# A decoder layer in one launch: parts of the output product fetched three ahead, expert outputs in tiles of their own, four splits moved to GpSimd

## The chip, the cores and the metric

The kernel runs on one core of one Trainium2 chip. The metric is the device time of one launch in microseconds (us), as the median of several runs. A core has five engines with an instruction queue each: TensorE (PE, matrix products; its weight loads are listed apart as PEld), VectorE (DVE), ScalarE (ACT), GpSimd (POOL) and SyncE (SP, which here issues most DMA transfers). An engine works through its queue in order; a semaphore wait holds everything behind it on that engine.

## What is computed

A decoder layer over 16 batches of 100 tokens of width 512 (1600 tokens), with an encoder context of 361 tokens for each batch, to float32's accuracy. Cut to what matters:

```python
x = layernorm(x + self_attention(x))                 # 16 heads of 32, causal
q, k, v = x @ Wq + bq, ctx @ Wk + bk, ctx @ Wv + bv  # 16 query heads, 4 key/value heads, width 128
o = softmax(rms(q) @ rms(k).T / sqrt(128) + mask) @ v
x = layernorm(x + o @ Wo)                            # Wo: 2048 x 512

logits = x @ router_w + router_b                     # 8 experts
vals, idx = top_k(logits, 2)
g = softmax(vals)
h = silu(x @ expert_w[e] + expert_b[e])              # for the two experts e of each token
y = x + (sum of g * h) @ proj_w + proj_b
x = layernorm(x + norm_w * y / rms(y))
```

## The kernel before, in words

**Accuracy.** PE multiplies float32r numbers. Each float32 operand is held as a `Pair` of two float32r tiles, high and low. `split` (L120) makes it: the high part is a copy on ScalarE (L124), the low part is source less high on VectorE or GpSimd (L127). `mm3` (L129) makes a product of two pairs from three matmuls (high-high, high-low, low-high; L131, L132, L133).

**Order of the work.** The kernel is written in the Tile framework. Python code emits operations in an order written out by hand. A planner then puts each engine's instructions into an order by a timeline that it estimates; semaphores are put in where tiles depend on one another. A pool has a fixed number of buffers for each tag; a new tile waits until the last readers and writers of the buffer that it takes are done. A pool that is opened in memory that a closed pool held waits likewise for the users of that memory.

**Stages.** Self attention (to about 350 us); its output product and the cross attention's queries (to about 600); cross attention (to about 1136); its output product with layer norm and router; experts; the weighted sum, projection and last norms.

**Cross attention.** For each batch and each of four groups of four heads: `x_scores` (scores of a head, L131 to L133; mask and maximum on VectorE, L679; exponential on ScalarE, L690; sums' reciprocal; normalisation on GpSimd, L692), `x_turn` (transposes of a chunk of encoder tokens, L700, then a split), `x_attend` (product with values; then the group's output goes to the DRAM scratch `od`, laid out by tiles of 128 tokens). The steps of two neighbouring groups are interleaved by a hand-written list. In batches before the last, the keys and values of the next batch are projected among them.

**Output product.** There are 13 tiles of tokens (the last has 64) and four groups of `Wo`, so 52 parts. Tiles 0 to 9 come tile by tile; of the last three (`TAIL`) the parts come by weight group. `d_load(i)` fetches a part from `od` by a DMA on SP (L755) into tile `of` and splits it into the pair `ot`; the low part goes to VectorE for odd `i`, to GpSimd for even `i`. `of` and `ot` have two buffers each, in pool `d_in`. `d_part(i)` issues its 12 matmuls of 128x512 into a PSUM bank (`acc`). `d_norm` (L779) adds the residual and normalises; `d_turn` transposes the normalised tile (L865) for the router. The first four parts are issued among the groups of the last batch; the others come in the main loop (L1252), which loads part i+1 and then multiplies part i. Weights of experts are fetched and split among them (`load_expert`; low parts `WL` on GpSimd).

**Router.** `d_logits` adds a tile's products with the router weights. `choose` takes each token's two experts. At the cut (`CUT`, tile 9) `settle` and `slots` work out, from the first nine tiles, the expert's tokens for 11 slot tiles of 128 tokens each, in many small VectorE operations that end in `is_in` (L1156); small products on PE (L1171) make the index lists. The other slots are settled after the last tile.

**Experts.** There are 32 slot tiles. `e_gather` (L1195) fetches a slot's 128 tokens by an indirect DMA on GpSimd's queue into tile `xs` (pool `k_x`, five buffers). `e_turn` transposes it (four PE transposes, L1206) and splits the result; `e_product` issues 12 matmuls with the weights of the slot's expert (`ph`); `e_out` adds the bias on VectorE (L1230), with its result written over the gathered tile `xs`, applies Silu on ScalarE (L1231), and SP writes the tile to the DRAM scratch `ysd` (L1232). For the weighted sum, rows of `ysd` are gathered for each tile of tokens (`y`, L1377, on GpSimd's queue).

Of the kernel before, what the change touches and what calls it, by code (L numbers as in the profile page):

```python
# [29 lines left out]
NG = B // GB  # L30
GT = GB * S
TT = [(t, min(128, T - t)) for t in range(0, T, 128)]  # tiles of all tokens
# [5 lines left out]
def pieces(t0, n):  # L38
    """The batches that tokens t0 to t0 + n lie in: (batch, its token, offset, count)."""
    out, t = [], t0  # L40
    while t < t0 + n:
        b, r = divmod(t, S)
        m = min(S - r, t0 + n - t)
        out.append((b, r, t - t0, m))
        t += m
    return out


class Pair:
    """A float32 array as the exact sum of two that float32r holds."""  # L50
# [12 lines left out]
def tile_decoder_layer(  # L63
# [29 lines left out]
    # Exp and Ln of one table serve both attentions.  # L93
# [26 lines left out]
    def split(dst, src, high=None, low=None):  # L120
        """dst, a pair, from src."""
# [7 lines left out]
    def mm3(out, a, b, start, stop):  # L129
        """The product of two pairs, to float32's accuracy."""  # L130
# [8 lines left out]
    def rsqrt(v, p, n, name, p_=None):  # L139
        """1 / sqrt(v), from the activation tables, with one Newton step."""  # L140
# [33 lines left out]
    # Eight slots of 512 rows by 512 columns, each a pair: weights, and what fits  # L174
    # beside them.
# [9 lines left out]
    def split_rows(dst, src, name, high=None, low=None):  # L185
        """Weights from DRAM into a pair, by rows."""
# [48 lines left out]
    def chunk(n, c, queue=None):  # L235
        """Weights from DRAM, 128 columns (of queries or keys) or rows (of values)."""
# [18 lines left out]
    # Keys of four heads, each in its own block of rows and of columns.  # L255
# [8 lines left out]
    # Added to negated scores: zero up to the diagonal, BIG past it.  # L264
# [35 lines left out]
    def self_q(g, c):  # L300
# [3 lines left out]
        # The scores come out negated and scaled.  # L304
# [71 lines left out]
    def self_attend(g, c, r):  # L376
# [3 lines left out]
        # Of each head's rows only its own columns are its output.  # L380
# [48 lines left out]
    LA = 3  # items that scores are ahead by  # L429
    extra = {}  # what comes with an item  # L430
# [1276 lines left out]
```

## Time and profile before

| what | value |
|---|---|
| three runs | 1482.58, 1488.05, 1488.45 us; median 1488.05 |
| span of the profiled execution (its own time is not listed beside it) | 1484.0 us |
| mean granted PE clock | 0.972 |
| attention's last groups, 1078.0 to 1136.5 | PE busy 58.50 of 58.5 us |
| first output tiles, 1136.5 to 1180 | PE busy 35.76 of 43.5 us |
| output tiles, 1180 to 1226 | PE busy 44.78 of 46 us |
| the cut, 1226 to 1270 | PE busy 33.49 of 44 us |
| experts among the second settling, 1270 to 1319 | PE busy 45.64 of 49 us |
| experts, 1319 to 1396 | PE busy 65.64 of 77 us |
| experts and weighted sums, 1396 to 1440 | PE busy 42.07 of 44 us |
| the end, 1440 to 1484 | PE busy 23.23 of 44 us |

The span runs from the first to the last instruction of one profiled execution; it lies within the range of the three runs. "Granted clock" is the share of its full clock that the throttle let PE have. The profile also tells, for each idle stretch of an engine, which instruction or transfer released it ("<-"): a line such as "acc<-WH,ot_l" gives output and inputs of an instruction by the program's names.

### The profile page before, as it was taken

To read this page: it belongs to the slowest core of one execution; us is meant where nothing else is said; L and a number is where in the kernel's file an instruction comes from. 1 tells how busy PE (TensorE), PEld (TensorE's weight loads), DVE (VectorE), ACT (ScalarE), POOL (GpSimd) and SP (SyncE) were. 2 spreads that over 40 slices of the span, in tenths; PEclk is the share of its full clock that TensorE was granted. 3 is DMA by queue.
4 is the path that set the end of the run, shared out by engine and by line. 5 is a ranking of instruction groups with operands and counts; after the bars stand their busy time and mean duration, and the time that the engine had idled before them with its cause. 6 is when DMAs were issued, how large, how long until landed. Compare 5 with 4: busy or idle time off the path is not lost.

```text
span 1484.0 us, 24770 instructions
## 1 busy us (share of the span) xinstructions
PE 1391.4 (94%) x7248; PEld 1139.8 (77%) x7248; DVE 1018.2 (69%) x3523; ACT 813.3 (55%) x2164; POOL 731.9 (49%) x853
## 2 busy tenths in 40 slices
PE   7999999999999999999999999999999898798985
PEld 6777786788877888788788788788887676576763
DVE  5775766677676777777777677677745558752698
ACT  5766877444444566566666566566654233332453
POOL 6455545534424555455655555555544444442643
PEclk9999999999999999999999999999999999899997
DMA  4011015456544222122322322321435645666774
GB/s 130 34 46 62 22 36 145 144 142 118 125 97 92 74 65 80 44 64 64 89 61 64 87 63 63 93 60 45 99 107 142 207 164 159 191 213 184 253 232 146
DMA packets 197875, 159.77 MB, mean 108 GB/s; under 512 B 133322, under 2 KB 152878, under 8 KB 197742
## 3 DMA queue, kind: packets, MB, share of 16 engines
q1 hardware_dynamic: 187904, 137.83, 33.7%
q0 software_dynamic: 4576, 14.95, 3.3%
q10 hardware_dynamic: 5262, 5.41, 1.3%
q8 instruction: 60, 0.98, 0.3%
q14 instruction: 73, 0.60, 0.1%
HBM read 107.16 MB, written 50.99 MB: 107 GB/s over the span
## 4 chain that ended last, share of the span: by engine, by line
PE 67%; DVE 17%; DMA 7%; issue 4%; ACT 3%; POOL 1%; SPq 1%; DVEq 0%; POOLq 0%; ACTq 0%
PE pv L131 4%; PE pv L132 4%; PE pv L133 4%; PE pq L131 4%; PE ptp L700 4%; PE pq L132 4%; PE pq L133 3%; PE s L131 3%; PE s L133 3%; PE s L132 3%; PE pk L131 3%; PE pk L133 3%; PE pk L132 3%; DVE ksq L639 2%; PE av L383 2%
## 5 line engine op out<-in xcount | busy, mean ns | idle before, releaser
L692 POOL TENSOR_SCALAR p<-p,sums 100x361 f32<-100x361 f32 x256 | 146.7, 577 | 107.7 <-DVE sums L691 88.7
L679 DVE CUSTOM_DVE_ANT_0 p<-s,nmask 100x361 f32<-100x361 f32 x256 | 133.5, 527 | 73.6 <-PE s L133 71.5
L690 ACT ACTIVATE p<-p,nm 100x361 f32<-100x361 f32 x256 | 153.4, 602 | 47.2 <-DVE nm L679 44.1
L127 DVE TENSOR_TENSOR pT_l<-ptp,pT_h 128x400 fp32r<-128x400 f32 (+1 forms) x192 | 107.4, 567 | 58.3 <-ACT pT_h L124 58.1
L124 ACT CAST pT_h<-ptp 128x400 fp32r<-128x400 f32 (+1 forms) x192 | 91.5, 488 | 33.4 <-PE ptp L700 32.8
L700 PE MATMUL ptp<-ident,p 100*128 100x100 f32 (+1 forms) x768 | 108.2, 253 | 0.1
L700 PEld LDWEIGHTS ptp<-ident,p 100*128 100x128 f32 (+1 forms) x768 | 95.9, 152 | 15.5 <-POOL p L692 4.2
L127 POOL TENSOR_TENSOR cT_l<-cf,cT_h 128x512 fp32r<-128x512 f32 (+1 forms) x48 | 54.4, 1134 | 97.2 <-ACT cT_h L124 95.9
L133 PE MATMUL acc<-WH,ot_l 128*128 128x512 f32 (+1 forms) x208 | 86.2, 415 | 8.4 <-DVE ot_l L127 5.4
L131 PE MATMUL acc<-WH,ot_h 128*128 128x512 f32 (+1 forms) x208 | 85.8, 413 | 3.5 <-ACT ot_h L124 3.5
L127 POOL TENSOR_TENSOR WL<-qf,WH 128x400 fp32r<-128x400 f32 x64 | 67.3, 1051 | 43.5 <-ACT WH L124 39.7
L131 PE MATMUL s<-kT_h,WH 128*100 128x362 f32 x256 | 88.7, 357 | 0.0
L131 PE MATMUL av<-pT_h,WH 128*128 128x400 f32 (+1 forms) x192 | 76.7, 400 | 8.2 <-ACT pT_h L124 8.2
L132 PE MATMUL acc<-WL,ot_h 128*128 128x512 f32 (+1 forms) x208 | 84.4, 406 | 0.0
L133 PE MATMUL s<-kT_h,WL 128*100 128x362 f32 x256 | 84.1, 329 | 0.0
L132 PE MATMUL s<-kT_l,WH 128*100 128x362 f32 x256 | 83.7, 327 | 0.0
L131 PE MATMUL pq<-WH 128*128 128x512 f32 (+1 forms) x208 | 82.3, 396 | 0.1
L132 PE MATMUL pq<-WL,WH 128*128 128x512 f32 (+1 forms) x208 | 81.6, 394 | 0.5 <-POOL WL L127 0.5
L551 POOL TENSOR_TENSOR qs<-qs,r_q 128x512 f32<-128x512 f32 (+1 forms) x52 | 54.3, 1075 | 54.5 <-DVE r_q L155 25.5
L131 PE MATMUL pv<-WH,cT_h 128*128 128x512 f32 (+1 forms) x192 | 80.3, 418 | 0.8 <-DVE WL L127 0.8
L639 DVE CUSTOM_DVE_ANT_0 ksq<-ks 128x128 f32<-128x128 f32 (+1 forms) x192 | 78.3, 408 | 2.4
L360 POOL TENSOR_TENSOR p<-p,rinv 100x400 f32<-100x400 f32 x64 | 54.2, 855 | 51.8 <-DVE rinv L359 37.3
(349 smaller groups left out, 4407.3 us busy)
## 6 DMA issues: line engine op xcount, KB each, us to landing
qf<-qd SPq DMA_DIRECT2D x64, 200.0 KB, 2.6
of<-od SPq DMA_DIRECT2D x48, 256.0 KB, 3.5
cf<-in_ctxT SPq DMA_DIRECT2D x16, 722.0 KB, 4.2
eb<-in_expert_b SPq DMA_DIRECT2D x32, 256.0 KB, 3.8
ysd<-xs SPq DMA_DIRECT2D x32, 256.0 KB, 4.1
f_e<-in_expert_w SPq DMA_DIRECT2D x30, 256.0 KB, 4.5
f_wq<-in_Wq SPq DMA_DIRECT2D x16, 256.0 KB, 4.0
f_wo<-in_Wo SPq DMA_DIRECT2D x16, 256.0 KB, 4.6
```

The lines of the kernel that those rows point to most:

```text
L124: nc.scalar.copy(dst.h, src)
L127: low.tensor_tensor(dst.l, src, dst.h.bitcast(FP), ALU.subtract)
L131: nc.tensor.matmul(out, a.h, b.h, start=start, stop=False)
L132: nc.tensor.matmul(out, a.h, b.l, start=False, stop=False)
L133: nc.tensor.matmul(out, a.l, b.h, start=False, stop=stop)
L360: nc.gpsimd.tensor_tensor(p, p, rinv.unsqueeze(2).to_broadcast([S, 4, S]), ALU.mult)
L551: nc.gpsimd.tensor_tensor(qr[:, hs, :], qr[:, hs, :], rs[:n, hs].unsqueeze(2).to_broadcast([n, GR, HD2]), ALU.mult,)
L639: nc.vector.tensor_tensor_reduce(out=sq[:n], in0=kr[:, h, :], in1=kr[:, h, :], scale=1.0, scalar=0.0, op0=ALU.mult, op1=ALU.add, accum_out ...
L679: nc.vector.tensor_tensor_reduce(out=p, in0=sc[:, :SE], in1=nmask, scale=1.0, scalar=BIG, op0=ALU.add, op1=ALU.min, accum_out=nm,)
L690: nc.scalar.activation(p, p, AF.Exp, bias=nm, scale=-1.0, accum_out=sh)
L692: nc.gpsimd.tensor_scalar(p, p, sh, 1.0, ALU.mult, ALU.mult)
L700: nc.tensor.transpose(pt[:n, h, :], probs[h][:, c0 : c0 + n], ident[:S, :S])
```

## The change

Three things are changed, all after the cross attention. Comments are taken out too, and lines move by some.

1. `d_load` is divided. `d_fetch(i)` issues the DMA from `od`; `d_load(i)` splits what was fetched. In the main loop parts are fetched up to three ahead (`AHEAD`, with a counter `begun`). Odd parts are fetched into a second pool `d_in2` of two buffers, opened just before the main loop; even parts into `d_in`, as before. In the attention's last batch each fetch stands directly before its split.
2. The low split goes to GpSimd for every part of tiles 9 and 10, odd ones too (`by_pool`); so four more splits are on GpSimd. (`CUT` is defined further up for that.)
3. `e_out` writes into a tile `h` of its own (two buffers in pool `ebb`), not over `xs`; `xs` has four buffers, not five.

```diff
+    AHEAD = 3
+    CUT = NT - 4
...
+    def d_fetch(i):
+        t, g = parts[i]
+        n = TT[t][1]
+        p = inp["d2"] if "d2" in inp and i % 2 else inp["d"]
+        of = p.tile([128, GR, 128], FP, name=f"of_{t}_{g}", tag="of")
+        nc.sync.dma_start(of[:, :, :n], od[t][:, g * GR : (g + 1) * GR, :n])
+        OF[t, g] = of
+
     def d_load(i):
         t, g = parts[i]
         n = TT[t][1]
-        p = inp["d"]
-        of = p.tile([128, GR, 128], FP, name=f"of_{t}_{g}", tag="of")
-        nc.sync.dma_start(of[:, :, :n], od[t][:, g * GR : (g + 1) * GR, :n])
-        OT[t, g] = pair(p, [128, GR, 128], f"ot_{t}_{g}", tag="ot")
-        split(OT[t, g][:, :, :n], of[:, :, :n], low=nc.vector if i % 2 else nc.gpsimd)
+        of = OF.pop((t, g))
+        OT[t, g] = pair(inp["d"], [128, GR, 128], f"ot_{t}_{g}", tag="ot")
+        by_pool = i % 2 == 0 or CUT <= t < NT - TAIL + 1
+        split(
+            OT[t, g][:, :, :n], of[:, :, :n], low=nc.gpsimd if by_pool else nc.vector
+        )
...
-    xsp = pool(fin, "k_x", 5, side="right")
+    xsp = pool(fin, "k_x", 4, side="right")
...
     def e_turn(i):
-        xs = XG[i]
+        xs = XG.pop(i)
...
     def e_out(i):
         ph = PH.pop(i)
-        h = XG.pop(i)
+        h = ebb.tile([128, D], FP, name=f"h_{i}", tag="h", bufs=2)
         nc.vector.tensor_tensor(h, ph, EB.pop(i), ALU.add)
         nc.scalar.activation(h, h, AF.Silu)
         nc.sync.dma_start(ysd[i * 128 : (i + 1) * 128, :], h)
...
+    d2 = ExitStack()
+    inp["d2"] = pool(d2, "d_in2", 2)
+    begun = HEAD * NKV + 1
     for i in range(HEAD * NKV, len(parts)):
         t, g = parts[i]
+        while begun < min(i + 1 + AHEAD, len(parts)):
+            d_fetch(begun)
+            begun += 1
         if i + 1 < len(parts):
             d_load(i + 1)
...
+    d2.close()
     d_i.close()
```

More of the change, by code (lines that the diff above doesn't have):

```diff
@@ L739, in tile_decoder_layer @@
     order = [(b, g) for b in range(B) for g in range(NKV)]
-    OT, X1 = {}, {}
+    OT, OF, X1 = {}, {}, {}
+    AHEAD = 3
+    CUT = NT - 4
     def d_open():
@@ L798, in tile_decoder_layer @@
                 d_open()
+                d_fetch(0)
                 d_load(0)
             for j in range(HEAD * g, HEAD * (g + 1)):
+                d_fetch(j + 1)
                 d_load(j + 1)
@@ L898, in tile_decoder_layer @@
     NSL = NE + (2 * T - NE) // 128
-    CUT, EARLY = NT - 4, 11
+    EARLY = 11
     assert EARLY <= 2 * CUT - (NE - 1)
```

## The prediction, made before the result was known

> **What bounds the kernel now.** I read the page first: TensorE (PE) is busy 94% of the span and leads its chain (67%), so only time in which PE idles or is throttled can be won, and most of that lies after 1136 us, where the slices fall from 9 to 8 and 7.
>
> ```profile
> span 1484.0 us, 24770 instructions
> PE 1391.4 (94%) x7248; PEld 1139.8 (77%) x7248; DVE 1018.2 (69%) x3523; ACT 813.3 (55%) x2164; POOL 731.9 (49%) x853
> PE   7999999999999999999999999999999898798985
> PEclk9999999999999999999999999999999999899997
> ```
>
> Then the windows view, by stage (columns: stretch, length, busy PE, PEld, DVE, ACT, POOL, granted clock, DMA share, GB/s). Rows: the attention's last five head groups, the first output tiles, the router's cut, the experts' main run.
>
> ```profile
> 1078.00:1136.50 58.50, 58.50 (x319) 50.58 (x318) 26.39 (x77) 32.01 (x77) 26.91 (x30) 1.00 0.46 119
> 1136.50:1180.00 43.50, 35.76 (x172) 27.31 (x172) 27.17 (x88) 13.26 (x31) 22.79 (x24) 0.98 0.62 195
> 1226.00:1270.00 44.00, 33.49 (x167) 23.00 (x167) 39.46 (x110) 13.05 (x25) 21.84 (x18) 0.93 0.47 151
> 1319.00:1396.00 77.00, 65.64 (x297) 51.38 (x298) 26.09 (x40) 25.45 (x47) 31.45 (x32) 0.93 0.70 225
> ```
>
> PE is full until 1136.5, then idle 7.75, 10.5 and 11.4 us in the rows that follow. The waits of PE from 1080 us on name the releasers (total, times, longest):
>
> ```profile
> PE pte L1206 <- DMA xs<-x2d,idx: 8.4, 7, 3.2
> PE acc L133 <- DVE ot_l L127: 5.4, 4, 3.8
> PE gb L1171 <- DVE is_in L1156: 4.1, 2, 3.4
> PE acc L131 <- ACT ot_h L124: 3.5, 3, 1.6
> PE acc L133 <- POOL ot_l L127: 2.4, 1, 2.4
> ```
>
> So parts that are split late cost 11.3 us (rows two, four, five) and gathered tokens that land late 8.4. Why the gathers are late, the chain and GpSimd's timeline tell (chain: start, duration, piece):
>
> ```profile
> 1315.18 0.61 DVE xs L1230
> 1315.81 0.64 ACT xs L1231
> 1316.47 4.54 DMA ysd<-xs
> ```
>
> ```profile
> 1307.26 1.05 POOL L1195 DMA_INDIRECT xs<-x2d,idx  x1 [12.79 <-DMA ysd<-xs]
> ```
>
> A gather refills a buffer from which an expert output was written, so it waits until that write has landed; GpSimd stood still 12.79 us here, and 24.4 us in all between 1296 and 1400.
>
> [...]
> - [...] after gaps of 1.7 and 3.2 us the clock in 10-us windows from 1320 reads .83, .95, .88, 1.00, .83. So a closed gap gives back some clock too.
> - [...] a 128x6 integer operation of 0.19 us takes 1.23 and ends with GpSimd's:
>
> ```profile
> 1238.58 1.29 POOL L127 TENSOR_TENSOR ot_l<-of,ot_h 128x512 fp32r<-128x512 f32 x1
> 1238.67 1.23 DVE L1044 CAST ri<-rj 128x6 int32<-128x6 f32 x1
> ```
>
> - [...] The trace: the low split takes 1.287 us on GpSimd, 0.691 on VectorE.
>
> **The change, part by part.** Base: the profiled execution. Nothing but its span, 1484.0, is given for it; the median 1488.05 lies 4.05 above, and I carry that on.
>
> *1, the attention loses its filler.* The order of the built programs is equal on PE up to about 1078 us. Then it parts. The second fetch pool lies in memory over the last attention's probabilities. The first odd part fetched there, (1,1), so waits for PE's transposes of the last head group (L700) and GpSimd's normalisation (L692). The 143 output-product matmuls of tiles 1 to 4 that stood between the last five head groups stand behind the last `av` product in the changed order. Back to back they start 0.2333 us apart (1080.04, 1080.28, 1080.51), so they move 143 x 0.2333 = 33.4 us, which is no loss in itself. What remains of the row of 58.5 us is 25.1 us of attention, 5.0 us per group. But the chain within it was hidden:
>
> ```profile
> 1122.66 0.53 PE L700 MATMUL ptp<-ident,p 100*105 100x100 f32 x4
> 1123.22 0.49 ACT L124 CAST pT_h<-ptp 105x400 fp32r<-105x400 f32 x1 [2.34 <-PE ptp L700]
> 1123.75 0.57 DVE L127 TENSOR_TENSOR pT_l<-ptp,pT_h 105x400 fp32r<-105x400 f32 x1 [3.67 <-ACT pT_h L124]
> ```
>
> From a chunk's transposes to its products 1.7 us pass (0.53 + 0.49 + 0.57 and hops). With two banks in turn the pace is about 1.15 us for a chunk against 0.85 of PE work: 15 chunks x 0.3 = 4.5 us. The last group has no scores of a next one beside it, some 3 us. Idle: **+7.5**, bounds 3 (the loads overlap fully) and 25 (nearly serial: a group takes its 5 us of engine work twice, 10 us). Clock: PE would be used 25/32.5 = 77%, as from 1160 to 1190, where 10-us windows read 1.00, .93, .90: some 5% of 32.5, **+1.5**.
>
> *2, the parts fetched early (A: 1142 to 1178).* These 7.75 us of waits on splits (the 2.4 on GpSimd's among them) were caused by fetches of 3.4 us (median landing; issue waits for a freed buffer of two) with one part of lookahead. With three parts ahead (four buffers) they go. New is one bubble: the fetch of (1,1) starts after the last group's transposes, 3.5 us + 0.65 for the high part and a hop gives 4.3 us, of which PE fills 2.0 with products, and the low part costs 0.35 more: 2.65. Net **-5.1**. SP issues no more transfers than before (0.32 us each), only earlier, so SP costs nothing. Of the wait of 1.22 us at 1209 (L865, behind tile norms that queue after splits) half goes: **-0.6**.
>
> *3, four low splits to GpSimd (tiles 9 and 10), at the cut.* PE idles 10.5 us, nearly all from 1240 to 1268: 1.55 + 3.76 on splits, 3.39 on `is_in`. VectorE is busy 39.5 of 44 us with the chain from the logits of tile 8 (1226.4) to `is_in` (1268.2); this 41.8 us chain ends last. Earlier splits do not shorten it. It begins about 2.2 us earlier, since the matmuls in front stand about ten places later in the order; it loses 4 x 0.69 = 2.8 us of splits, of which three lie in it: 2.1. [...] 4 x 1.287 x 0.75 = 3.9 at the most, 2.8 if one falls outside. 2.2 + 2.1 - 2.8 = **-1.5**, bounds -4.5 (no hold) and +1.5 (no early start, full hold). The waits on splits are then filled by waits on `is_in`, not gained twice. GpSimd is busy 21.8 of 44 us there: 5.1 more it can take; behind the moved splits on its queue stand weights' low splits, which are needed after 1270; were one needed sooner, it would cost its delay, 1.29 for each split ahead.
>
> *4, outputs apart from gathered tokens (1319 to 1396).* The gather then waits for the four transposes, as soon as the tokens are turned. Of the 11.4 us idle new waits take back about 1.4 (an output tile is one of two, so the add of slot i waits for the write of slot i-2: 0.61 + 0.64 + 4.54 + hops 0.1 = 5.9 us for two slots, 2.95 a slot, against 12 x 0.2333 + 0.63 = 3.43 of PE; the rare longer write shows): **-10.0**. The five 10-us windows from 1320 lose 10 x (.17 + .05 + .12 + 0 + .17) = 5.1 us to the clock; closing gaps returns two thirds: **-3.5**. Bounds of both together: 0 (rival 1) and -16.5. What is late next is PE itself, then GpSimd's y gathers. Four gather buffers for five cost nothing: a buffer is now held for gather (4.3) and turn only, two slots. The end (1440 to 1484) shifts as a block: 0.
>
> *Sum:* +7.5 + 1.5 - 5.1 - 0.6 - 1.5 - 10.0 - 3.5 = -11.7: the span goes from 1484.0 to 1472.3, the time to 1488.05 - 11.7 = 1476.4.
>
> **The rivals.**
> *Rival 1: the ring of two outputs takes the place of the gather's wait.* For: the decision point is a write of 2 x 3.43 - 1.39 = 5.5 us, and the chain shows 4.30, 4.54, 4.66 but also 5.51 and, on gathers, 7.22; traffic becomes denser. At 7 us a slot takes 4.2, about today's pace, and step 4's 13.5 us go: 1476.4 + 13.5 = 1489.9, no change.
> *Rival 2, slower: the attention's end runs nearly serially without its filler.* Price: idle 25 and clock 5 in place of 7.5 and 1.5, 21 more: 1497.4. The other steps win 20.7 us together, so the time is slower than before from 20.7 us of idle and clock in this place on, and by over 0.5% from 28.1. For: ACT, DVE and POOL have some 22 us of work each in the five groups, and every hop is bare. Against: the order interleaves two groups.
> *Rival 3: the gaps close wholly.* Idle in the attention 4, all 11.4 + 5.1 of the experts, the cut -4.5: 3.5 + 3.0 + 3.0 = 9.5 less: 1466.9.
> *The change doesn't do what it says:* the depth of three is useless for the first odd part, since its pool overlaps the probabilities. That is inside step 1 and no case of its own.
>
> **How the numbers follow.** Forecast 1476.4 (own range 1468 to 1483): 0.42. Rival 1: 0.26. Rival 2: 0.20. Rival 3: 0.12. A measurement tells 0.5% (7.4 us) from no change, so faster is below 1480.6: 0.32 of the forecast, all of rival 3, 0.03 of rival 1 = 0.47; slower is above 1495.5: 0.18 of rival 2 and 0.04 of rival 1 = 0.22; the rest 0.31. The range 1465 to 1497 leaves out about half of rival 2 and half of rival 3, 0.16.
>
> **What would show it.** Step 1: the last five head groups in about 33 us with 7 to 8 of PE idle; over 46 would be rival 2. Step 2: no wait of PE on `ot` over 1 us but one of about 2.7 after the last `av`. Step 3: logits of tile 8 to `is_in` about 41 us. Step 4: no wait of POOL's xs for ysd, slots at 3.5 us; 4 us with waits of the add on ysd would be rival 1. I am wrong if the experts' stretch does not shrink by 10 us, or the attention's end idles over 15.

## The result, and the profile after

Over 20 runs of each the changed kernel takes 1488.85 us (median; 1483.83 to 1494.95), the kernel before 1485.16 us (1478.26 to 1490.58). The ratio is 1.0026, with a 95% interval of 1.0014 to 1.0039: 0.26% slower, inside the 0.5% that the prediction called no change. The forecast was 1476.4, faster by 0.8%. The profiled execution took 1484.11 us, the second fastest of the 20, with a span of 1482.4.

The page of the changed kernel shows the same sums as before (the same 7248 matmuls, PE busy 94%); the slices with 7 and 8 are still there, in other places:

```profile
span 1482.4 us, 24725 instructions
PE 1388.4 (94%) x7248; PEld 1138.3 (77%) x7248; DVE 1017.6 (69%) x3519; ACT 815.0 (55%) x2164; POOL 736.8 (50%) x857
PE   7999999999999999999999999999989998799985
PEclk9999999999999999999999999999999998899997
```

**Where to count from.** The span of this trace is 1.6 us shorter than that of before, though the kernel is slower. The reason lies ahead of the change: PE's order is the same up to the first product of a part of `Wo` (the first `acc`), and still that product starts at 1057.5 us in the trace of before, at 1052.3 in this one, and between 1052.2 and 1065.0 in the eighteen traces of this study. So all stages below are counted from the first `acc`; else what a trace lost or won by chance before 1060 us would be read as an effect of the change.

Each kernel was traced twice (the second traces are runs "changed again" and "before again" below). Mean of the two, and what the prediction's steps put at the same places:

| stage (us from one milestone to the next) | before | changed | measured | predicted |
|---|---|---|---|---|
| first `acc` to the logits of tile 8 | 169.5 | 170.35 | +0.9 | +1.1 (9.0 - 5.7 - 2.2) |
| logits of tile 8 to the end of `is_in` | 41.75 | 45.65 | +3.9 | +0.7 (2.8 - 2.1) |
| to the end of the second settling | 46.8 | 52.1 | +5.3 | 0 |
| to the end of the last expert product | 118.55 | 107.75 | -10.8 | -13.5 |
| to the end of the span | 47.95 | 55.15 | +7.2 | 0 |
| sum | 424.55 | 431.0 | +6.5 | -11.7 |

The sums of the two traces differ by 3.9 us for the kernel before (426.5, 422.6) and by 1.8 for the changed one, so +6.5 in the traces and +3.7 in the medians do not contradict each other. Nearly all of the 3.9 lies in the experts (120.6 and 116.5 us): a stage of a single trace can be off by some 4 us.

The windows view of the changed kernel (columns as before: stretch, length, busy PE, PEld, DVE, ACT, POOL, granted clock, DMA share, GB/s; the attention's end, first output tiles, cut, experts, end):

```profile
1078.00:1110.00 32.00, 27.57 (x155) 23.58 (x154) 17.43 (x69) 20.55 (x56) 13.40 (x25) 0.89 0.48 101
1136.50:1180.00 43.50, 41.29 (x188) 32.67 (x188) 24.41 (x63) 15.07 (x30) 22.69 (x17) 0.96 0.54 173
1226.00:1270.00 44.00, 30.71 (x119) 21.22 (x118) 35.13 (x90) 12.68 (x24) 24.07 (x20) 0.81 0.44 132
1319.00:1396.00 77.00, 71.22 (x356) 55.94 (x355) 30.77 (x57) 27.40 (x48) 37.29 (x37) 0.96 0.78 247
1440.00:1484.00 44.00, 21.70 (x76) 14.72 (x76) 30.87 (x98) 16.00 (x34) 10.75 (x8) 0.74 0.33 110
```

The experts' row did what was hoped: 356 PE instructions in 77 us, 297 before. The cut got worse: PE busy 30.7 of 44 us, 33.5 before, at a clock of .81, before .93. The waits of PE from 1080 us on (total, times, longest) name the two waits in it that are new in size, the first two rows. The third row is the pause after the attention:

```profile
PE gb L1183 <- DVE is_in L1168: 6.5, 1, 6.5
PE acc L133 <- DVE ot_l L127: 6.5, 1, 6.5
PE acc L131 <- ACT ot_h L124: 3.9, 2, 3.6
PE pp L131 <- ACT cp_h L124: 3.2, 1, 3.2
PE ptx L877 <- DVE x L167: 2.4, 2, 1.6
PE pte L1218 <- DMA xs<-x2d,idx: 2.3, 2, 1.4
```

The wait for gathered tokens fell from 8.4 us to 2.3 (last row). GpSimd's own waits from 1296 to 1400 have no row of `xs` on `ysd` any more, which had been 24.4 us; it now waits for the transposes that free a buffer, as part 3 intends:

```profile
POOL xs L1207 <- PE pte L1218: 33.8, 14, 5.3
```

### The profile page after: what moved, and what is told of

It is laid out like the page before. It is cut to its first block, busy times and chain, and to the rows that moved or that the text cites. A ratio compares the mean times of both kernels' runs of the same rounds, so it can differ in the third digit from the quotient of the medians.

```text
span 1482.4 us, 24725 instructions
## 1 busy us (share of the span) xinstructions
PE 1388.4 (94%) x7248; PEld 1138.3 (77%) x7248; DVE 1017.6 (69%) x3519; ACT 815.0 (55%) x2164; POOL 736.8 (50%) x857
## 4 chain that ended last, share of the span: by engine, by line
PE 67%; DVE 17%; DMA 6%; ACT 4%; issue 3%; POOL 1%; SPq 1%; another core or an unknown queue 0%; ACTq 0%; DVEq 0%; POOLq 0%
PE pv L131 4%; PE pv L133 4%; PE pv L132 4%; PE pq L131 4%; PE pq L133 3%; PE pq L132 3%; PE ptp L700 3%; PE s L131 3%; PE s L133 3%; PE s L132 3%; PE pk L131 3%; PE pk L133 3%; PE pk L132 3%; PE acc L133 2%; DVE ksq L639 2%
## 5 line engine op out<-in xcount | busy, mean ns | idle before, releaser
L127 POOL TENSOR_TENSOR cT_l<-cf,cT_h 128x512 fp32r<-128x512 f32 (+1 forms) x48 | 54.4, 1134 | 92.8 <-ACT cT_h L124 91.7
L132 PE MATMUL acc<-WL,ot_h 128*128 128x512 f32 (+1 forms) x208 | 84.7, 407 | 0.0
L131 PE MATMUL pk<-WH,cT_h 128*128 128x512 f32 (+1 forms) x192 | 78.1, 407 | 1.4 <-DVE ks L630 1.4
```

What stands on the lines that cost most here:

```text
L127: low.tensor_tensor(dst.l, src, dst.h.bitcast(FP), ALU.subtract)
L131: nc.tensor.matmul(out, a.h, b.h, start=start, stop=False)
L132: nc.tensor.matmul(out, a.h, b.l, start=False, stop=False)
```

## The experiments

**Three theories, which may hold together.** *The pool*: the second pool's place is the cost; its first fetch waits for the attention, and what follows is late. *The cut*: splits moved to GpSimd, or splits still on VectorE, meet the settling. *The end*: part 3's gain is given back after the experts, where something else is late. One table for all runs; stages are counted as above, "settled" takes in the second settling, ratios are of medians to the kernel before on the same chip, with 95% intervals.

| kernel | first `acc` to logits 8 | to `is_in` | settled | experts | end | sum | ratio |
|---|---|---|---|---|---|---|---|
| before | 168.9 | 41.8 | 46.9 | 120.6 | 48.3 | 426.5 | |
| before again | 170.1 | 41.7 | 46.7 | 116.5 | 47.6 | 422.6 | .9999 (.9979 to 1.0018) |
| changed | 169.7 | 45.7 | 52.1 | 107.1 | 55.5 | 430.1 | 1.0026 (1.0014 to 1.0039) |
| changed again | 171.0 | 45.6 | 52.1 | 108.4 | 54.8 | 431.9 | 1.0010 (.9987 to 1.0032) |
| e1: part 3 alone | 170.4 | 42.0 | 46.9 | 110.5 | 54.8 | 424.6 | .9970 (.9956 to .9983) |
| e2: part 2 alone | 168.3 | 40.7 | 49.1 | 121.9 | 48.2 | 428.2 | .9983 (.9968 to .9997) |
| e3: changed less part 2 | 172.1 | 41.5 | 49.0 | 108.8 | 54.8 | 426.2 | 1.0009 (.9992 to 1.0026) |
| e5: e1, last fetches on SP | 169.6 | 42.1 | 46.4 | 110.2 | 56.7 | 425.0 | .9969 (.9955 to .9984) |
| e6: e1, one Newton step | 169.2 | 42.2 | 45.2 | 112.7 | 53.1 | 422.5 | .9965 (.9950 to .9980) |
| e7: changed, late splits on GpSimd | 171.1 | 38.8 | 57.9 | 105.8 | 53.7 | 427.3 | .9996 (.9975 to 1.0017) |
| e8: changed, second pool from part 17 | 173.2 | 45.3 | 52.2 | 109.1 | 59.4 | 439.2 | 1.0036 (1.0021 to 1.0051) |
| e9: e1, last fetches first | 169.3 | 41.9 | 46.7 | 111.7 | 57.9 | 427.5 | .9975 (.9963 to .9986) |
| e10: parts 2 and 3 | 166.3 | 41.1 | 48.1 | 111.0 | 54.7 | 421.2 | .9918 (.9894 to .9941) |
| e16: e10 again | 167.2 | 43.0 | 45.1 | 107.1 | 58.1 | 420.5 | .9943 (.9922 to .9963) |
| e11: e10, last fetches first | 166.1 | 40.4 | 48.5 | 111.3 | 59.2 | 425.5 | .9961 (.9947 to .9975) |
| e12: changed, second pool from part 25 | 162.9 | 45.8 | 51.4 | 109.3 | 55.1 | 424.5 | .9986 (.9971 to 1.0001) |
| e13: e10, tail's scaling on GpSimd | 166.0 | 43.0 | 46.5 | 105.2 | 55.1 | 415.8 | .9929 (.9909 to .9949) |
| e14: e12 less part 2 | 169.7 | 42.1 | 46.9 | 105.2 | 56.3 | 420.2 | .9959 (.9945 to .9973) |

### One part at a time: e1, e2, e3, and the changed kernel again

e1 is the kernel before with part 3 alone:

```diff
-    xsp = pool(fin, "k_x", 5, side="right")
+    xsp = pool(fin, "k_x", 4, side="right")
...
-        xs = XG[i]
+        xs = XG.pop(i)
...
-        h = XG.pop(i)
+        h = ebb.tile([128, D], FP, name=f"h_{i}", tag="h", bufs=2)
```

> The kernel before with part 3 of the change alone (outputs in tiles of their own, four gather buffers); the order of work is that of before until the experts. Theory (each gain is handed back behind it: the experts end earlier, but the last norms, for which VectorE is full, then take longer): the last expert product ends 7 to 10 us earlier than before counted from its first, the stretch from there to the end grows by 5 to 8, the time is 1 to 4 us below before (ratio 0.997 to 0.9995). Rival (the end moves with the experts, and all of the loss is made at the cut): 7 to 10 us below before, ratio 0.993 to 0.995.

e2 is the kernel before with part 2 alone:

```diff
-        split(OT[t, g][:, :, :n], of[:, :, :n], low=nc.vector if i % 2 else nc.gpsimd)
+        by_pool = i % 2 == 0 or NT - 4 <= t < NT - TAIL + 1
+        split(OT[t, g][:, :, :n], of[:, :, :n], low=nc.gpsimd if by_pool else nc.vector)
```

> The kernel before with part 2 alone (the low splits of all parts of tiles 9 and 10 on GpSimd). Theory (at the cut these splits cost more than they save, as GpSimd is slower and VectorE's small operations wait for it): logits of tile 8 to the last is_in of the first settling takes 2 to 5 us longer than the 40.5 of before, the time is 2 to 4 us above before (ratio 1.001 to 1.003). Rival (the cut's loss comes from the fetches and the order behind them, not from these splits): the chain is as long as before or 1.5 us shorter, the ratio 0.999 to 1.000.

e3 is the changed kernel less part 2, and e4 the changed kernel once more, beside them:

```diff
-        by_pool = i % 2 == 0 or CUT <= t < NT - TAIL + 1
+        by_pool = i % 2 == 0
```

> The changed kernel without part 2 (low splits alternate as before). Theory: the cut gives back 3 to 5 us against the changed kernel, some of which the end swallows: 2 to 4 us below the changed kernel, about the time of before (ratio to before 0.999 to 1.001). Rival: as the changed kernel, ratio 1.0025.

> The changed kernel as it is, for a second trace beside the first (which fell on one of its fastest runs) and for its time on the same chip as the other three. Theory and rival: ratio 1.0026; the second trace tells which stage holds the 3 to 5 us between its fastest and its middle runs: the cut by the theory, as its waits are the longest; the last norms by the rival.

Each of parts 2 and 3 alone makes the kernel faster (.9983, .9970; for part 2 the interval's upper end is .9997, so barely). The theory for e2, a longer chain and a slower kernel, was wrong. Part 1 added to part 3 takes the ratio from .9970 to 1.0009 (5.8 us at 1487). In e1 the experts win and the end loses nearly as much. The chain from the logits to `is_in` is long only where parts 1 and 2 are together: 45.7 and 45.6, against 40.7 in e2 and 41.5 in e3. So the cut is a cost, but as a meeting of two parts, and part 3 gives back at the end by itself. The second trace of the changed kernel places none of the time between its fastest and its middle runs at the cut or in the last norms: its span is 12.0 us longer, and 10.2 of these lie ahead of the first `acc`.

### Where the second pool opens: e8, e12, e14

e8 and e12 are the changed kernel with one part of lookahead, as before, until the given part; the second pool opens there (17 in e8, 25 in e12). The attention so keeps its filler: the last `av` ends 79.0 us after the first `acc`, as before, and 48.3 in the changed kernel. The edit of e12 (e8 has 17, 16 and 15 where it has 25, 24 and 23):

```diff
-        p = inp["d2"] if "d2" in inp and i % 2 else inp["d"]
+        p = inp["d2"] if i % 2 and i >= 25 else inp["d"]
...
-    inp["d2"] = pool(d2, "d_in2", 2)
...
-        while begun < min(i + 1 + AHEAD, len(parts)):
+        if i == 24:
+            inp["d2"] = pool(d2, "d_in2", 2)
+        while begun < min(i + 1 + (AHEAD if i > 23 else 1), len(parts)):
```

> The changed kernel with the second fetch pool opened, and three parts fetched ahead, only from part 17 on; parts 5 to 16 use the first pool as before, so the output products stand among the attention's last head groups again. Theory (part 1 costs what the bare attention end and the bubble behind it cost, 0.8 + 3.6 us idle and some 2 us of clock, less what it wins later): the bubble after the last av product is gone, the parts are done 2 to 5 us earlier counted from the first part product, ratio to before 0.997 to 1.000. Rival (the cut's chain ends last whenever the parts arrive): gain before the cut, then longer waits in it, ratio 1.001 to 1.003.

> The changed kernel with the second fetch pool opened, and three parts ahead, only from part 25 on, some 20 us after the attention, when the memory that it lies over has long been given up; until then as before. Theory (the pause behind the attention is the wait for that memory): no wait over 3 us between the last av product and 30 us behind it, 40% of the part products within 2 us of before (95.9 us after the first), where e8 had 106.9; the cut as in the changed kernel; ratio to before 0.999 to 1.0015. Rival (fetching further ahead itself crowds the transfers or ScalarE's queue): the pause or a like one comes after part 25, and the ratio stays at 1.002 to 1.004.

e14 is e12 with the line of e3:

> e12 (second pool from part 25 on) without part 2. Theory (parts 1 and 2 collide at the cut: with the parts early, PE reaches the splits that stand on VectorE behind the settling sooner and waits longer, and the moved splits crowd GpSimd at that time): logits of tile 8 to the end of the first settling falls from 45.8 to 41 to 42.5 us, the first expert product comes 2 to 4 us earlier than in e12 (221.4 us after the first part product), ratio to before 0.995 to 0.9975. Rival (the early parts alone lengthen the settling): 44 to 46, ratio as e12, 0.9985.

First the changed kernel. By the prediction's reading the second pool lies over the attention's probabilities `p`. The trace agrees: two fetches leave SP's queue 0.06 us after PE's last transposes of `p` have ended (1098.23 + 0.53):

```profile
1098.23 0.53 PE L700 MATMUL ptp<-ident,p 100*105 100x100 f32 x4
1098.82 0.95 SPq L757 DMA_DIRECT2D of<-od  x2
```

The high part of what they bring starts at 1103.47, and PE has stood 3.56 us for it (the rows are shown under step 1 below).

e8 is no better than the changed kernel (1.0036). Its timeline shows a pause in another place:

```profile
1144.83 0.62 ACT L124 CAST ot_h<-of 128x512 fp32r<-128x512 f32 x1 [9.91 <-DMA of<-od]
1145.50 0.80 PE L131 MATMUL acc<-WH,ot_h 128*128 128x512 f32 x1 [5.11 <-ACT ot_h L124]
1156.76 1.66 PE L896 MATMUL gb<-rw,x2f 128*128 128x8 f32 x8 [2.36 <-DMA rw<-in_router_w]
```

Read it from the top: ScalarE stands 9.91 us for a fetch, PE 5.11 us for ScalarE, and then 2.36 us for the router's weights, whose fetch is issued on ScalarE's queue behind the late copy (at 1148.65). The filler is back and the cost stays, so the cost does not need a bare attention. But not all of the 9.91 us is a wait for memory: three fetches of parts leave SP's queue at 1133.64, 1135.59 and 1136.91, around the end of the last transposes of `p` (1134.40), together with six other transfers, and the DMA engines are at least 67% busy from 1134 to 1140 and full from 1140 to 1144. How much of the wait is memory and how much is this crowd, the trace does not tell. The theory for e8, a gain, was wrong. In e12 the memory has long been given up when the pool opens; no wait of PE after the attention is over 2.5 us up to the logits (the longest are 2.42 and 2.13), and the ratio is .9986, against 1.0026 and 1.0010 for the changed kernel: 0.2 to 0.4% faster. e14 against e3 is the same step without part 2: .9959 against 1.0009, 0.5%. Two pairs agree (in the traces' sums 431.0 against 424.5, and 426.2 against 420.2): opening the pool and looking ahead at once, and not from part 25 on, costs 6 to 7 us by the traces. The step moves three things together (the pool, the start of the lookahead, and the attention's filler); that the wait for the pool's memory is the largest of them is read from the rows above, and a pool in memory of its own was not tried.

Where it is lost, the windows view tells, over the same stretch counted from the first `acc` (20.7 to 84.7 us after it): first the changed kernel, then e12.

```profile
1073.00:1137.00 64.00, 58.77 (x311) 49.23 (x310) 34.39 (x104) 32.72 (x79) 27.02 (x37) 0.95 0.50 135
```

```profile
1075.40:1139.40 64.00, 61.96 (x331) 53.01 (x330) 30.64 (x89) 34.69 (x86) 29.18 (x32) 1.00 0.49 132
```

20 matmuls fewer in the same time, 20 x 0.2333 = 4.7 us: the pause of 3.56, and behind it a stretch in which the clock is .50 (from 1103 to 1107 us) and matmuls start 0.43 us apart (1105.16, 1105.59, 1106.01); over the row the clock is .95. The rest of the 6 to 7 us lies later and is not placed by one row.

e12 against e14 prices part 2 where part 1 is: 1.0027 times as long, and the chain to `is_in` 45.8 for 42.1, as e14's theory had it. Its first expert product, though, comes 223.0 us after the first `acc`, not 2 to 4 us ahead of e12's 221.4: what is won at the cut was lost before it (169.7 for 162.9). Without part 1, part 2 gains instead (e10 and e16 against e1). Whether part 1 is worth anything with its pool opened late is not settled: e14 has parts 1 and 3 and .9959, e1 has part 3 and .9970, and the intervals overlap.

### What stands at the cut: e7

The timeline of the changed kernel at the cut (start, duration, engine, line, operation; in brackets the idle time before it and what ended it):

```profile
1244.10 0.69 PE L133 MATMUL acc<-WH,ot_l 128*64 128x512 f32 x1 [6.48 <-DVE ot_l L127]
...
1248.23 0.62 ACT L124 CAST ot_h<-of 128x512 fp32r<-128x512 f32 x1 [11.35 <-PE acc L132]
1248.29 0.23 DVE L1142 SCALAR_TENSOR_TENSOR fills<-first,fills 128x72 f32<-128x72 f32 x1
...
1252.01 0.69 DVE L127 TENSOR_TENSOR ot_l<-of,ot_h 128x512 fp32r<-128x512 f32 x1 [3.49 <-ACT ot_h L124]
...
1257.19 7.89 DVE L1151 TENSOR_TENSOR last<-last,opn 128x8 f32<-128x8 f32 x9
...
1266.84 0.17 PE L1183 MATMUL gb<-is_in,named 128*128 128x11 f16 x1 [6.49 <-DVE is_in L1168]
```

It is a ring. A low split of tile 12 is queued on VectorE behind settling operations, so PE stands 6.48 us for it. PE is then late with the products that free `ot`, so ScalarE's next high part stands 11.35 us and the one after it waits for PE once more. VectorE reaches the operation on `fills` 26.3 us after the logits of tile 8 (before: 30.5), finds that high part missing and stands 3.49 us, with the rest of the settling queued behind the split. What follows then meets GpSimd's splits: nine operations on `last` take 7.89 us; before, five of them took 3.14 and the other four 0.77. So a lead of 4.2 us has become a lag of 3.9 at `is_in`. GpSimd's rows beside those nine:

```profile
1257.61 1.32 POOL L127 TENSOR_TENSOR ot_l<-of,ot_h 128x512 fp32r<-128x512 f32 x1 [0.54 <-ACT ot_h L124]
1258.88 3.74 POOL L127 TENSOR_TENSOR WL<-f_e,WH 128x512 fp32r<-128x512 f32 x3
```

The ring alone does not make the chain long. It stands, with nearly the same lead at `fills` (26.4 to 26.6 us after the logits), in the five kernels that have part 2 and not part 1 (e2, e10, e11, e13, e16): PE waits 6.7 to 6.9 us for the low split, VectorE 1.0 to 3.8 for the high part, and yet `is_in` comes after 40.4 to 43.0 us. What the four long chains (45.3 to 45.8: changed, changed again, e8, e12) have beside it is the slow stretch on `last`: its nine operations take 7.6 to 8.7 us there, summed, and 3.1 to 4.1 in the five. e2's rows of VectorE and GpSimd:

```profile
1260.64 1.17 DVE L127 TENSOR_TENSOR ot_l<-of,ot_h 128x512 fp32r<-128x512 f32 x1 [1.81 <-ACT ot_h L124]
1261.73 3.35 DVE L1140 TENSOR_TENSOR last<-last,opn 128x8 f32<-128x8 f32 x9
1266.44 1.48 POOL L127 TENSOR_TENSOR ot_l<-of,ot_h 128x512 fp32r<-128x512 f32 x1 [2.79 <-ACT ot_h L124]
```

GpSimd's next split comes when the nine operations are over, because ScalarE stood 3.67 us for its fetch (the copy starts at 1265.74, "<-DMA of<-od"). In the changed kernel the part has been fetched early: ScalarE's copy there (1256.91) waits 1.83 us for PE's products and for no fetch, GpSimd's split starts 35.6 us after the logits (37.6 in e2), and the splits run beside the nine. So the ring comes with part 2, and part 1's early fetch sets GpSimd's splits beside the end of the settling. The other way round, e3 and e14 have part 1 and slow operations on `last` (6.8 and 6.7 us) without the ring, and no longer chain (41.5, 42.1).

e7 takes the remaining low splits from tile 9 on off VectorE as well, so that none can stand in the settling:

```diff
-        by_pool = i % 2 == 0 or CUT <= t < NT - TAIL + 1
+        by_pool = i % 2 == 0 or CUT <= t
```

> The changed kernel with the low splits of the last four odd parts (of tiles 11 and 12) on GpSimd too, so that no split stands among VectorE's operations of the first settling. Theory (PE reaches the part early, its split stands on VectorE behind the settling, and VectorE then stands for a high part that PE's wait holds up): the waits of 6.5 us (PE for a low split on VectorE) and 3.5 us (VectorE for a high part) go, the settling ends 2 to 5 us earlier counted from the first part product, ratio to before 0.9985 to 1.0005. Rival [...]: it grows by 2 to 3 us more, ratio 1.003 to 1.005.

The chain to `is_in` shortens to 38.8 us, the shortest of all: without splits on VectorE there is no ring, and the nine operations on `last` run free (1.5 us). But PE then stands 9.2 us for `is_in`, and 46 matmuls of output products stand between the first settling and the second (34 in the changed kernel), so the first expert product comes 23.4 us after `is_in` instead of 12.8. Of the chain's 6.9 us the trace's sum keeps 3.7 (427.3 against 431.0); the ratio, .9996 against 1.0026 and 1.0010, is not clear of noise.

### Parts 2 and 3 without part 1: e10, e16

e10 is the kernel before with the edits of e1 and e2. e16 is the same again.

> Parts 2 and 3 of the change without part 1. Theory (part 1 is what loses: alone behind it the four splits cost 4 us at the cut, without it they win 1 to 2): e1 and e2 add up, ratio to before 0.9945 to 0.9965. Rival (parts 2 and 3 get in each other's way): 0.999 to 1.001.

> e10 as it is, beside e13 and on the same chip: its ratio rested on six runs. Theory (e1 and e2 add up, and the collision of parts 2 and 1 is gone): 0.992 to 0.9955, against 0.9918 measured and 0.9953 from the sum of e1 and e2. Rival (the first measurement was lucky): 0.9955 to 0.998.

Ratios of .9918 and .9943: e10's interval lies below that of every kernel without both parts, e16's overlaps some of them at its edge. So parts 2 and 3 without part 1 beat both kernels: some 0.7% faster than before, 0.8 to 1.0% faster than the changed kernel by its two ratios.

### Who takes part 3's gain back: e5, e6, e9, e11, e13

From the last expert product on, e1 needs 54.8 us where the kernel before needs 48.3. Two rows each of the windows view (the first 20 us after that product, and the rest), before and then e1:

```profile
1435.70:1455.70 20.00, 14.90 (x68) 10.84 (x68) 17.40 (x50) 10.81 (x20) 14.03 (x14) 1.00 0.88 285
1455.70:1484.00 28.30, 11.17 (x42) 7.34 (x40) 22.25 (x75) 10.00 (x23) 5.90 (x5) 0.73 0.24 82
```

```profile
1429.00:1449.00 20.00, 14.29 (x57) 10.03 (x56) 13.59 (x44) 10.49 (x19) 13.92 (x13) 0.91 0.85 268
1449.00:1484.00 35.00, 14.03 (x63) 9.43 (x61) 27.08 (x88) 12.02 (x27) 6.79 (x5) 0.82 0.23 80
```

A little more work is left over in e1: PE has 120 instructions instead of 110 (some 2 us at 0.2333 us each, an estimate), VectorE 40.7 us of work instead of 39.7. But VectorE stands idle 14.1 us of the time instead of 8.7. The bytes are nearly the same too (20 x 268 + 35 x 80 GB/s us = 8.16 MB, against 8.02), and the first 20 us run with the DMA engines 85 to 88% busy in both. The longest wait of VectorE there, in e1:

```profile
DVE z L1442 <- remote: 4.1, 1, 4.1
```

"remote" says that the trace does not show the releaser; the products that `z` reads ended 3.2 us earlier by their modelled ends. Before has no wait over 1.7 us there. But this wait is not the delay: e14 and e16 have part 3, no wait of VectorE over 2.1 us in the end, and ends as long (56.3, 58.1). Four suspects were tried.

*A late fetch of `z`*, issued on ScalarE's queue behind its other work (e5: on SP):

```diff
-            if not tail:
+            if not tail or t < LATE:
                 nc.sync.dma_start(dst[:n], src[:n])
```

> The kernel with outputs in tiles of their own (as in e1), and in the last norms the two fetches for token tile 7 (z from xbd, x from x2d) on SP's queue, where they stood on ScalarE's behind a copy that waits for TensorE. Theory A (what the end gives back is this late fetch: VectorE stood 4.1 us for z in e1): that wait is gone and the stretch from the last expert product to the end falls from 54.8 by 2 to 4 us; ratio to before 0.994 to 0.996 where e1 had 0.997. Theory B (the end is VectorE's backlog, the fetch only fills a pause that would come anyway): stretch within 1 us of e1, ratio 0.9965 to 0.9975.

*VectorE's backlog of norms* (e6 leaves two of three Newton steps of the inverse square root out of the last norms, some 7 us of VectorE's work, an estimate from 1.2 us for each of six norms):

```diff
-        for k in range(3):
+        for k in range(1):
```

> The kernel with outputs in tiles of their own (as in e1), and one Newton step for three in the reciprocal roots of the last norms before the tail: the kernel leaves out two refinement steps, 6 small VectorE operations (about 1.2 us) for each of some six norms, 7 us of VectorE work that lies among the experts. Theory B (VectorE's backlog is what the end is bound by): the time falls by 4 to 7 us against e1, ratio to before 0.992 to 0.9945. Theory A (a fetch behind a copy): at most 1.5 us, ratio 0.996 to 0.997.

*The order of ScalarE's queue, fetches first* (e9: the fetches of the last five tiles are written ahead of the gathers' users, not among them; e11: the same in e10):

```diff
     for t in range(REST + 1, LATE):
         f_load(t)
+    for t in range(LATE, NT):
+        f_load(t)
...
-            f_load(k + 2)
```

> The kernel with outputs in tiles of their own (as in e1); in the last norms the fetches of z and x for tiles 8 to 12 are written ahead of the sums, so that on ScalarE's queue the scaling of the gathered rows of tiles 10, 11 and 12 no longer stands behind the squares of tiles 8 and 9. Theory C (what the end gives back is this order on ScalarE: in e1 the scaling of tiles 11 and 12 ran 26.5 and 27.8 us after the last expert product, in before 17.0 and 21.9): they run before 22, the stretch from the last product to the end falls from 54.8 to 49 to 52 us, ratio to before 0.993 to 0.995. Rival (the gathers and fetches fill the DMA engines until 20 us after the last product, and what follows takes as long in any order): stretch within 1.5 us of e1, ratio 0.9965 to 0.9975.

> e10 with the tail's fetches ahead of the sums, as in e9; the version that the experiments point to so far. Theory C: ratio to before 0.990 to 0.993. Rival: as e10, 0.9945 to 0.9965.

*The order of ScalarE's queue, scaling elsewhere* (e13, from e10: the gathered rows of the last five tiles are scaled on GpSimd, so that a sum need not wait its turn on ScalarE):

```diff
+        if t < LATE:
...
+        else:
+            nc.gpsimd.tensor_scalar(
+                c[:n], c[:n], g1[:n, t : t + 1], 1.0, ALU.mult, ALU.mult
+            )
```

> e10 (parts 2 and 3) with the scaling of the gathered rows of tiles 8 to 12 on GpSimd, where it stood on ScalarE's queue behind the squares of tiles 8 and 9, which wait for TensorE. Theory C (that order is what the end gives back; in e10 the transfers were done some 19 us after the last expert product, the scaling of tiles 11 and 12 ran after 26.4 and 27.7): tile 11's scaling runs at 21 or before, the stretch from the last product to the end falls from 54.7 to 50 to 52 us, ratio to before 3 thousandths below e10 measured beside it. Rival (the transfers bound the end): stretch 54 to 56, ratio as e10.

e5: the fetch starts 7 us earlier and the wait stays, so the late fetch is not the cause (.9969, as e1's .9970):

```profile
1425.94 0.32 SPq L1400 DMA_DIRECT2D z<-xbd  x1
```

```profile
DVE z L1442 <- remote: 4.0, 1, 4.0
```

e6: the first of the last eight projections start as early as before again (6.2 us ahead of the last expert product, as 6.1 before and 1.8 in e1), and yet the end takes 53.1 us: 1.7 of 7 us arrive, no more than the PE work that stands ahead of that product again. VectorE's load is at most a small part. e9 and e11 make the end longer (57.9, 59.2). ScalarE in e9's end, its last issue of a fetch and the first scaling:

```profile
1445.48 0.45 ACTq L1402 DMA_DIRECT2D x<-x2d  x1
1445.98 0.72 ACT L1411 ACTIVATE y<-y,g 128x512 f32<-128x512 f32 x1 [8.95 <-DMA z<-xbd]
```

The scaling of tile 8 starts 18.8 us after the last expert product instead of 8.1. ScalarE issues these fetches itself: twelve of them stand in its queue from 1434.37 to 1445.93, and the scaling starts 0.05 us after the last. So these two runs put a new wait in the place of the old one, and tell nothing of the order of the transfers. e13 does what they meant to do: the last two scalings start 16.8 and 20.3 us after the product instead of 26.4 and 27.7, and the end stays at 55.1, between e10's 54.7 and e16's 58.1. ScalarE's order alone is not it either.

What the traces do show is where the delay has come in. The scalings of the last five tiles start 6.5, 7.7, 13.6, 17.0 and 21.9 us after the last expert product in before, 8.1, 10.4, 16.1, 26.5 and 27.8 in e1. The last projection ends at 32.5 and 38.6, and from there 14.5 to 16.3 us remain in each of the eighteen traces. Of the last seven projections the first starts at 0.4 in before and 3.5 in e1, and the six steps to the last take 29.1 and 32.2. So the last tiles' projections are late by 6 us, half of it at their start and half on the way, with no single wait that makes them so. This stays open.

## Why the prediction was wrong, step by step

The time lay in the range, but the sign forecast was wrong: -11.7 predicted, +3.7 in the medians, +6.5 in the traces. Neither of the two signs that the prediction named for being wrong appeared: the experts' stretch shrank by 10.8 us, and the attention's end idled 4.4 us. Both looked where the prediction had a price, and the loss is made elsewhere. The difference of 18.2 us in the traces is -0.2 (to the logits of tile 8), +3.2 (the cut), +5.3 (between the settlings), +2.7 (the experts) and +7.2 (the end).

**Step 1, the attention's end: cheaper than said; what costs is the pause behind it.** The last `av` ends 48.3 us after the first `acc`; 79.0 - 33.4 = 45.6 would be without loss, so the stretch lost 2.7 us in place of 9.0, with waits of 0.24, 0.36 and 0.19 us. Rival 2 (30 us here) is out. The pause after it was put at 2.65:

```profile
1103.47 1.14 ACT L124 CAST ot_h<-of 128x512 fp32r<-128x512 f32 x2 [2.25 <-DMA of<-od]
1104.12 0.69 DVE L127 TENSOR_TENSOR ot_l<-of,ot_h 128x512 fp32r<-128x512 f32 x1 [4.22 <-ACT ot_h L124]
1104.14 0.80 PE L131 MATMUL acc<-WH,ot_h 128*128 128x512 f32 x1 [3.56 <-ACT ot_h L124]
```

It is 3.56 us. 2.7 + 3.56 - 2.65 = 3.6 where the sum had 9.0. By the pairs e3/e14 and changed/e12 the early pool costs 6 to 7 us in all. The prediction saw the overlap of the pool with the probabilities and called it "inside step 1 and no case of its own"; with the pool opened at part 25 it is avoidable.

**Step 2, the parts fetched early: a reading that was too large, and a gain eaten up.** The 7.75 us was all of PE's idle time in the row of 1136.5 to 1180, and was taken for waits on splits. The waits of PE in that row that are for splits sum to 4.9 us:

```profile
PE acc L133 <- POOL ot_l L127: 2.4, 1, 2.4
PE acc L133 <- DVE ot_l L127: 1.6, 3, 0.7
PE acc L131 <- ACT ot_h L124: 0.9, 1, 0.9
```

The rest is for tile norms and the router. These 4.9 us went as said. But in their place stand the pause of 3.56 and a new wait of 2.1 us for the router's `place` on VectorE, so that all waits of PE from 1080 us to the logits sum to 8.9 us in both kernels. That +0.9 came where the sum had +1.1 is luck, as the errors of steps 1 and 2 hide one another: 2.7 + 3.56 = 6.3 us were lost, 2.3 came back because the logits' products stand ten places earlier (10 x 0.2333, as forecast; the traces have this wherever part 2 is, and nowhere else), and some 3 by the lookahead, where 7.75 + 0.6 had been put. What the lookahead is worth without the early pool is not settled: e12's logits come 162.9 us after the first `acc`, 3 to 5 ahead of the five kernels with part 2 and without part 1 (166.0 to 168.3), but e14, with the same lookahead, needs 169.7, as the kernels without parts 1 and 2 do (168.9 to 170.4); in its trace the clock from 1165 to 1180 is .77, behind a wait of 2.92 us.

**Step 3, the cut: wrong sign.** 2.8 us, an estimate of the author's for how much longer VectorE's small operations take beside the four moved splits (its factor of 0.75 stands in no trace), less 2.1 for the splits that VectorE loses, was a sum of durations. It took the waits between the engines as they were. With part 2 a low split on VectorE, a high part on ScalarE and PE's products wait for each other across the queues of three engines (6.48, 11.35 and 3.49 us in the rows of the changed kernel above); with part 1 beside it GpSimd's splits meet the end of the settling. The chain is 3.9 us longer, not 0.7; part 2 alone, in e2, makes it 1.0 shorter. PE's clock in this row is .81, with two gaps of 6.5 us, where before had .93 with gaps of 3.8 and 3.4. The nine operations on `last` take 0.88 us each beside GpSimd's splits; in before four of them, at a time when GpSimd was idle, took 0.19 each. The prediction counted longer operations only beside the four moved splits; beside the weights' splits behind them they are longer too: `first<-first,fills` took 1.22 us beside a split of `WL` (1253.99 in the changed kernel), 0.23 with GpSimd idle (1257.43 in before).

**Between the two settlings: +5.3, not foreseen, and mostly moved work.** The changed kernel has 273 PE instructions there, before 242. Some 24 of the difference are matmuls of 512 columns: 12 of an output product (34 from `is_in` on, before 22) and 12 of an expert product (98 have begun by the end of the stretch, before 86). 24 x 0.2333 = 5.6 us. The output products are about the ten that stood ahead of tile 8's logits before; the expert product is missing later. PE idles 4.2 us there, before 3.1.

**Step 4, outputs apart: the mechanism held, the size not.** The gather no longer waits for the write of an expert's output (24.4 us of GpSimd's waits to none), Rival 1's wait of the add on `ysd` occurs once with 1.9 us, and the stretch shrinks by 10.8 us; PE's clock from 1319 to 1396 is .96, before .93. 2.8 of the 10.8 (12 x 0.2333) are the expert product just named, so 8.0 are earned, where 13.5 were put. Four traces with part 3 have no such shift and no edit at the end (e1, e10, e14, e16: 84 or 85 matmuls of expert products by the end of the second settling); there the stretch takes 108.5 us on average, over the three traces without part 3 (before twice, e2) 119.7: 11.2 us. The kernel before by itself shows 120.6 and 116.5: the profiled execution, on which the 13.5 was worked out, was long in this stretch.

**"The end shifts as a block: 0" is the step that failed most.** Over the same traces the end takes 56.0 us on average with part 3 and 48.0 without. So of 11.2 us that part 3 wins among the experts, 8.0 are given back (some 2 of them the ten PE instructions that now stand behind the last expert product), and the 3 or so that stay agree with e1's ratio (0.0030 x 1485 = 4.5 us). The prediction looked for what is late next and named PE and GpSimd's `y` gathers, but gave it no price. The end was a place in which the profile of before showed PE busy 23 of 44 us: not bound by PE. This stretch did not move forward as PE's work ahead of it did; what holds it is open, as said above.

**The rivals.** None of the three with a chance was right. "The change doesn't do what it says" named the true place, the second pool over the probabilities, and was given neither a price nor a chance. The time of Rival 1 (1489.9, "no change") came closest, by another mechanism than its own. What came was a case that the prediction did not have: parts 2 and 3 each gain by themselves, part 2's gain becomes a loss beside part 1, and most of what part 3 wins among the experts is given back behind them.

## What to carry to other kernels

Before a pool is opened early so as to fetch ahead, ask who last uses the memory that it lands in: if that is the stage just ending, the first fetch waits for it, and with it the engines whose queues need what it brings (here PE stood 3.56 us). Price a gain in one stage only together with the stages after it: ask of the next one what binds it, and where it is not the engine that was sped up, a part of the gain may stay there (here 8.0 of 11.2 us). And try the parts of a change one by one: here two of three gained 0.7% together, and the third, as it stood, made of it a loss.

## What the runs showed of the hardware

- Behind the same order of PE's instructions, the first `acc` started between 1052.2 and 1065.0 us in eighteen traces, a spread of 12.8 us, more than any of the parts is worth. Only counting from a milestone close to the change made the traces comparable.
- VectorE operations of 128x72 took 0.23 us with GpSimd idle (1248.29 in the changed kernel), 1.31 and 1.22 us beside GpSimd's splits (1236.87 and 1253.99). So the time of a stretch with 102 VectorE operations (logits of tile 8 to `is_in` in the changed kernel) depended also on what GpSimd did beside them: the nine on `last` took 7.89 us there, 3.91 in before.
- Twelve fetches in ScalarE's queue took it from 1434.37 to 1445.93 us to issue in e9, and the scaling behind them started 0.05 us after the last: 18.8 us after the last expert product instead of 8.1.
- Behind PE's pause of 3.56 us in the changed kernel, the clock granted from 1103 to 1107 us is .50, and matmuls of 512 columns start 0.43 us apart instead of 0.2333.
